# All pairwise products of each row: the whole input loaded by SyncE ahead of the first store, in place of loads that GpSimd issues between the stores

## The chip, the cores and the metric

The kernel runs on one core of one Trainium2 chip. The metric is the device time of one execution in microseconds (us). Three timed runs of the kernel before gave 1261.1, 1260.95 and 1261.11 us; the median is 1261.1 us.

## The reference

For each of 4096 rows of 256 float32 numbers, the reference forms all products of two elements of the row and keeps the upper triangle, diagonal included:

```
dot = jnp.einsum('bi,bj->bij', inputs, inputs)     # inputs: 4096 x 256, f32
iu, ju = jnp.triu_indices(256)
return dot[:, iu, ju]                               # 4096 x 32896, f32
```

The input is 4.19 MB, the output 538.97 MB.

## The kernel before

**Layout.** The 4096 rows stand on the 128 partitions, 32 consecutive rows on each, so that a partition's input is one run of 32 KB. `REPEAT = 2` rows of each partition are worked on at a time (512 input numbers, `each`). The 32,896 output columns are cut into three pieces of 10,944, 10,944 and 11,008 columns (`spans`). One piece for 2 rows on 128 partitions is one store of 256 runs of 43,776 or 44,032 bytes, about 11.2 MB. A pass `h` handles four rows of each partition, 4 KB of input per partition, in six pieces (`p` from 0 to 5); there are eight passes, so 48 pieces in all. `ROUND` says which 4 KB of the input each pass takes.

**Buffers.** Two output buffers, `o0` and `o1` (the list `places`), take turns. A piece is written into one of them by VectorE (helper `vector`, the multiplications of line 281) and GpSimd (helper `gpsimd`, line 382) together, while SyncE's store of the other buffer is on its way. SyncE issues each store in program order (helper `sync`, line 410) once the counter `v_done` says that the piece is complete. VectorE's first multiplication of a piece waits until the earlier store from that buffer has landed (semaphore `free`); GpSimd's first waits for VectorE's (`go`).

**The head.** The first two pieces are done differently (`ahead`). VectorE (line 242) and ScalarE (line 309) write the first piece in blocks, each of which is stored as soon as both are through with it. `FIRST = [704, 1984, 3968, 6592]` gives the borders, so the blocks are 704, 1280, 1984, 2624 and 4352 columns wide. Before block number `DIRECT` VectorE copies the input rows to PSUM (`xp`, line 237). TensorE, which has nothing else to do, counts the landings of the blocks' stores (`head`) and then frees `o0` (line 448).

**The input.** All of it stays in one buffer, `xt` (named `x` in the trace). SyncE loads three parts ahead of the first store (lines 440 and 441): 2 KB per row of the layout, that is per partition, for the first two rows; 8 KB, passes 1 and 2, as 256 runs of 4 KB; 2 KB, the rest of pass 0. Passes 3 to 7 are loaded by GpSimd between its pieces (helper `late`, lines 327 and 354, with the table `LATE`): passes 3 and 4 together (unit `ONE`) and passes 6 and 7 together (unit `TWO`) each in four transfers over 20, 45, 3 and 60 partitions, pass 5 (`EVEN`) in one transfer over all 128. Ahead of most of these GpSimd issues a transfer of 2 to 12 partitions by 2 x 128 bytes into `marks`, a buffer that no instruction reads (helper `mark`). `HAD` makes GpSimd wait, one or two pieces later, until a unit has landed.

Of the kernel before, what the change touches and what calls it, by code (L numbers as in the profile page):

```python
# [8 lines left out]
F32 = mybir.dt.float32  # L9
# [3 lines left out]
P = 128  # L13
UNIT = 64
REPEAT = 2
PIECES = 3
EDGE = 32
ROUND = [0, 2, 5, 1, 3, 7, 4, 6]
GAP = 32
ONE, EVEN, TWO = (3, 4), (5,), (6, 7)  # L20
LATE = [
    ((1, 3), ONE, [((5,), 20), ((6,), 45)]),
    ((2, 3), ONE, [((2,), 3), ((12,), 60)]),
    ((3, 3), EVEN, [((), 128)]),
    ((4, 3), TWO, [((8, 9), 20), ((6,), 45)]),
    ((5, 3), TWO, [((2,), 3), ((12,), 60)]),
]
HAD = [((2, 5), ONE, 4, 0), ((4, 5), EVEN, 1, 0), ((5, 5), TWO, 4, 9)]
HELPED = 1
HELP = 16.5  # L30
MARK = 32
PLACES = 2
SETS = 5
PASS = 6
# [1 line left out]


LATER = 1.0
FIRST = [704, 1984, 3968, 6592]
DIRECT = 3  # L40
COPY = 700


# [94 lines left out]
def window(ap: bass.AP, free: list) -> bass.AP:  # L138
    return bass.AP(ap.tensor, ap.offset, [list(ap.ap[0]), *free])
# [3 lines left out]
def kernel(  # L143
# [15 lines left out]
    nc = tc.nc  # L159
    n, d = x.shape  # L160
    width = out.shape[1]
    each, groups = REPEAT * d, n // (P * REPEAT)
    rounds = PASS // PIECES
    passes = groups // rounds
# [6 lines left out]
    x_in = x.rearrange("(p g) d -> p (g d)", p=P)  # L171
    x_out = out.rearrange("(p h q r) c -> h q p r c", p=P, q=rounds, r=REPEAT)

    pool = ctx.enter_context(tc.tile_pool(name="all", bufs=1))
    edge = pool.tile([P, EDGE], F32, name="edge")
    places = [pool.tile([P, REPEAT, slot], F32, name=f"o{k}") for k in range(PLACES)]
    xt = pool.tile([P, passes, rounds * each + GAP], F32, name="x")
    xv = pool.tile([P, each + 1], F32, name="xv")
    marks = pool.tile([P, 2, 2 * MARK], F32, name="marks")

    xp = ctx.enter_context(tc.tile_pool(name="psum", bufs=1, space=bass.MemoryType.PSUM)).tile([P, each], F32, name="xp")
    ctx.enter_context(tc.tile_critical())  # L182
# [1 line left out]
    def semaphore(name: str):  # L184
        return ctx.enter_context(nc.semaphore(name))

    free = [semaphore(f"free{k}") for k in range(PLACES)]
    head, v_done, a_done, go = (semaphore(s) for s in ("head", "v_done", "a_done", "go"))
    loaded = [semaphore(f"loaded{k}") for k in range(3)]
    far, marked = {u: semaphore(f"far{u[0]}") for u in (ONE, EVEN, TWO)}, semaphore("marked")  # L190

    def take(engine, sem, value: int):
        engine.wait_ge(sem, value).then_inc(sem, -value)  # L193
# [2 lines left out]
    g_done, x_copied, warm = (semaphore(s) for s in ("g_done", "x_copied", "warm"))  # L196

    def x_of(h, q: int) -> bass.AP:
        return xt[:, bass.ds(h, 1), q * each : (q + 1) * each].rearrange("p o d -> p (o d)")

    def blocks(p: int, ahead: bool):

# [99 lines left out]

    def scalar(pieces: range):

        xa = xt[:, 0, :each]
        for p in pieces:
            for _, _, block, _, lo in blocks(p, True):
                todo = [
                    nc.scalar.activation(  # L309
                        places[p][:, r, at - lo : at - lo + length],  # L310
                        xa[:, r * d + j : r * d + j + length],
                        AF.Copy,
                        scale=xa[:, r * d + i : r * d + i + 1],
                    )
                    for i, j, at, length in block
                    for r in range(REPEAT)
                ]
                if todo:
                    todo[-1].then_inc(a_done, 1)
                else:  # L320
                    nc.scalar.sem_inc(a_done, 1)

    flat = xt.rearrange("p h d -> p (h d)")

    def mark(lo: int, hi: int):
        of = window(x_in[lo:hi], [[2 * MARK, 2], [1, MARK]])
        nc.gpsimd.dma_start(marks[lo:hi, :, :MARK], of).then_inc(marked, 16)  # L327

    def inputs(of_passes: tuple, rows: slice, lo: int = 0, hi: int = rounds * each) -> tuple:
        first, last = of_passes[0], of_passes[-1]  # L330
        ends = []
        for ap, at, step in (
            (flat, first * (rounds * each + GAP), (last - first) * (rounds * each + GAP)),
            (x_in, ROUND[first] * rounds * each, (ROUND[last] - ROUND[first]) * rounds * each),
        ):
            dims = [[step, 2], [1, hi - lo]] if step else [[1, hi - lo]]
            ends.append(window(ap[rows, at + lo :], dims))
        return tuple(ends)

    def late(h, p: int):  # L340
        at, rows = 0, {}
        for (begun, piece), of_units, parts in LATE:
            with ExitStack() as when:
                if p == piece:
                    when.enter_context(nc.gpsimd.If(h == begun))
                for steps, count in parts:
                    row = rows.get(of_units, 0)
                    rows[of_units] = row + count
                    for step in steps:
                        if p == piece:  # L350
                            mark(at, at + step)
                        at += step
                    if p == piece:
                        nc.gpsimd.dma_start(*inputs(of_units, slice(row, row + count))).then_inc(far[of_units], 16)  # L354
        for (had, piece), of_units, count, count_of_marks in HAD:
            if p == piece:
                with nc.gpsimd.If(h == had):
                    nc.gpsimd.wait_ge(far[of_units], 16 * count)
                    if count_of_marks:
                        nc.gpsimd.wait_ge(marked, 16 * count_of_marks)  # L360
                    nc.gpsimd.drain()

    def gpsimd(h, pieces: range, ahead: bool, done: int = 0, turns: int = 0) -> tuple:
        if ahead:
            take(nc.gpsimd, go, 1)
            nc.gpsimd.memset(xv[:, each:], 0.0).then_inc(g_own, 1)  # L366
            nc.gpsimd.tensor_copy(xv[:, :each], x_of(0, 0)).then_inc(g_own, 1)  # L367
            done += 2
            nc.gpsimd.wait_ge(g_own, done).then_inc(x_copied, 1)
        for p in [HELPED] if ahead else pieces:  # L370
            place = places[p % PLACES]
            block, lo = helped(p) if ahead else next((block, lo) for _, _, block, _, lo in blocks(p, False))
            turns += not ahead
            if not ahead:
                late(h, p)
            order = interleave(block)
            waits = schedule(order)
            counted = {*waits.values()}
            number = {k: done + 1 + c for c, k in enumerate(sorted(counted))}
            for k, ((i, j, at, length), m, _) in enumerate(order):  # L380
                at -= lo
                ins = nc.gpsimd.tensor_tensor(  # L382
                    place[:, :, at : at + m * length],
                    window(xv[:, j:], [[d, REPEAT], [1, m], [1, length]]),
                    window(xv[:, i:], [[d, REPEAT], [1, m], [0, length]]),
                    ALU.mult,
                )
                if k == 0 and not ahead:
                    ins._wait_ge(go, turns)
                elif k in waits:  # L390
                    ins._wait_ge(g_own, number[waits[k]])
                if k in counted:
                    ins.then_inc(g_own, 1)
            done += len(counted)
            ins.then_inc(g_done, 1)
        return done, turns

    def sync():
        done = ahead_done = 0
        for turn in range(passes * PASS):  # L400
            h, p = divmod(turn, PASS)
            ahead, place = turn < AHEAD, places[p % PLACES]
            parts = list(blocks(p, ahead))
            for lo, hi, *_, base in parts:
                done += 1
                if ahead:
                    ahead_done += 1
                    nc.sync.wait_ge(a_done, ahead_done)
                to = x_out[ROUND[h], p // PIECES, :, :, base + lo : base + hi]
                store = nc.sync.dma_start(to, place[:, :, lo:hi])  # L410
                store._wait_ge(v_done, done)
                store.then_inc(free[p % PLACES] if len(parts) == 1 else head, 16)
        for sem, count in ((v_done, done), (a_done, ahead_done)):
            nc.sync.sem_inc(sem, -count)
# [22 lines left out]
            nc.vector.wait_ge(v_own, counts[0]).then_inc(v_done, 1)  # L437
        settle(engine, counts)

    for (of_passes, lo, hi), sem in zip((((0,), 0, each), ((1, 2), 0, 2 * each), ((0,), each, 2 * each)), loaded):  # L440
        nc.sync.dma_start(*inputs(of_passes, slice(0, P), lo, hi)).then_inc(sem, 16)
    nc.vector.memset(edge, 0.0).then_inc(warm, 1)  # L442
    take(nc.scalar, warm, 1)
    nc.scalar.activation(edge[:, :1], edge[:, 1:2], AF.Copy, scale=edge[:, 2:3])  # L444
    for engine in (nc.vector, nc.scalar, nc.gpsimd):
        engine.wait_ge(loaded[0], 16)
    take(nc.tensor, head, 16 * (len(FIRST) + 1))
    nc.tensor.sem_inc(free[0], 16)
# [35 lines left out]
```

## Time and profile before

| what | value |
|---|---|
| timed runs, median (lowest to highest) | 1261.1 us (1260.95 to 1261.11) |
| profiled execution: span from the first to the last instruction | 1259.5 us |
| VectorE busy | 822.7 us (65%), 1236 instructions |
| GpSimd busy | 763.5 us (61%), 1149 instructions |
| ScalarE busy | 27.1 us (2%), 74 instructions |
| moved by DMA | 543.24 MB, mean 431 GB/s |
| HBM read and written | 4.21 MB and 538.97 MB |

One execution was profiled. Its time is known as the span; the median of the timed runs is 1.6 us longer than the span. The core has 16 DMA engines, which carry out the transfers of all queues: q1 is SyncE's queue, q0 is GpSimd's, q14 fetches instructions. In the views, DVE is VectorE, ACT is ScalarE, POOL is GpSimd, SP is SyncE; a "q" behind an engine is its sequencer, which waits and issues. `L281` is line 281 of the kernel.

### The profile page before, as it was taken

What the parts mean: (1) busy time and instruction counts of PE and PEld (TensorE: products, weight loads), DVE (VectorE), ACT (ScalarE), POOL (GpSimd) and SP (SyncE); (2) the same over time, 40 slices, a digit from 0 to 9 for tenths busy, and PEclk for the clock granted to TensorE, in tenths of its full rate; (3) what the DMA queues carried; (4) which work ended last, traced back from release to release, by engine and by line L of the source; (5) the groups of instructions that cost most, each with busy time, mean ns of one, the idle gap of its engine ahead of it and who ended that gap; (6) DMA issues with size and microseconds to landing.
All of it is one profiled execution on the core that took longest, in us unless ns stands there. A gap on an engine that the chain in (4) does not pass through costs nothing. (4 is left out here: it accounts for less than half of the span.)

```text
span 1259.5 us, 2827 instructions
## 1 busy us (share of the span) xinstructions
DVE 822.7 (65%) x1236; ACT 27.1 (2%) x74; POOL 763.5 (61%) x1149
## 2 busy tenths in 40 slices
DVE  8767657676576665766657675676656766567650
ACT  8000000000000000000000000000000000000000
POOL 5666647665476654766558665576645765467650
DMA  9999999999999999999999999999999999999998
GB/s 396 433 445 423 443 427 433 433 442 427 434 436 432 430 434 435 434 430 441 427 438 433 426 438 427 441 428 438 431 437 428 440 428 437 432 435 432 438 431 380
DMA packets 15911, 543.24 MB, mean 431 GB/s; under 512 B 1440, under 2 KB 1440, under 8 KB 3360
## 3 DMA queue, kind: packets, MB, share of 16 engines
q1 hardware_dynamic: 14704, 540.54, 99.3%
q0 software_dynamic: 1200, 2.64, 0.5%
q14 instruction: 7, 0.06, 0.0%
HBM read 4.21 MB, written 538.97 MB: 431 GB/s over the span
## 5 line engine op out<-in xcount | busy, mean ns | idle before, releaser
L281 DVE TENSOR_TENSOR o<-xv,xp 128x504 f32<-128x504 f32 (+59 forms) x1175 | 791.2, 746 | 398.1 <-DMA out_dram<-o 268.2
L382 POOL TENSOR_TENSOR o<-xv 128x64 f32<-128x64 f32 (+61 forms) x1125 | 751.6, 709 | 450.0 <-DVE o L281 449.8
L309 ACT ACTIVATE o<-x 128x198 f32<-128x198 f32 (+34 forms) x72 | 25.5, 448 | 0.8 <-DMA x<-in_r_inputs_dram 0.8
L260 DVE COPY xp<-x 128x512 f32 x15 | 10.3, 685 | 0.0
L242 DVE TENSOR_TENSOR o<-x,xp 128x470 f32<-128x470 f32 (+18 forms) x19 | 9.7, 585 | 0.0
L242 DVE TENSOR_TENSOR o<-x 128x510 f32<-128x510 f32 (+9 forms) x10 | 5.7, 647 | 2.5 <-DMA x<-in_r_inputs_dram 2.5
L258 DVE COPY xv<-x 128x512 f32 x15 | 6.5, 433 | 0.5
L366 POOL MEMSET xv<- 128x1 f32 x1 | 0.1, 99 | 10.3 <-POOLq L193 10.3
L327 POOL DMA_DIRECT2D marks<-in_r_inputs_dram x9 | 5.7, 637 | 0.4 <-issue 0.3
L354 POOL DMA_DIRECT2D x<-in_r_inputs_dram x9 | 5.5, 615 | 0.0
L444 ACT ACT_TABLE_LOAD x1 | 1.3, 1283 | 1.2 <-ACTq L193 1.2
L442 DVE MEMSET edge<- 128x32 f32 x1 | 0.1, 85 | 1.0 <-SPq L182 1.0
L237 DVE COPY xp<-x 128x512 f32<-128x512 f32 x1 | 0.7, 686 | 0.0
L367 POOL COPY xv<-x 128x512 f32<-128x512 f32 x1 | 0.6, 611 | 0.0
L444 ACT ACTIVATE edge<-edge 128x1 f32<-128x1 f32 x1 | 0.3, 295 | 0.0
L471 POOL MEMSET const-float32-0.0<- 128x1 f32 x1 | 0.1, 99 | 0.2 <-issue 0.2
L471 POOL MEMSET const-bfloat16-1.0<- 128x1 bf16 x1 | 0.1, 103 | 0.0
L471 POOL MEMSET const-uint8-127<- 128x1 uint8 x1 | 0.1, 103 | 0.0
L471 POOL MEMSET const-float32-1.0<- 128x1 f32 x1 | 0.1, 99 | 0.0
## 6 DMA issues: line engine op xcount, KB each, us to landing
out_dram<-o SPq DMA_DIRECT2D x31, 10944.0 KB, 35.2
out_dram<-o SPq DMA_DIRECT2D x16, 11008.0 KB, 32.8
out_dram<-o SPq DMA_DIRECT2D x1, 4352.0 KB, 13.8
out_dram<-o SPq DMA_DIRECT2D x1, 2624.0 KB, 9.4
out_dram<-o SPq DMA_DIRECT2D x1, 1984.0 KB, 7.2
out_dram<-o SPq DMA_DIRECT2D x1, 1280.0 KB, 5.2
x<-in_r_inputs_dram SPq DMA_DIRECT2D x1, 1024.0 KB, 4.9
x<-in_r_inputs_dram POOLq DMA_DIRECT2D x2, 480.0 KB, 29.2
```

The source lines that it names most:

```text
L237: nc.vector.tensor_copy(xp, x_of(h, 0)).then_inc(v_own, 1)
L242: ins = nc.vector.tensor_tensor(place[:, :, at - lo : at - lo + length], window(x_of(h, 0)[:, j:], [[d, REPEAT], [1, 1], [1, length]]), wi ...
L258: ins = nc.vector.tensor_copy(xv[:, :each], x_of(h, p // PIECES))
L260: nc.vector.tensor_copy(xp, x_of(h, p // PIECES)).then_inc(v_own, 1)
L281: ins = nc.vector.tensor_tensor(place[:, :, at : at + m * length], window(xv[:, j:], [[d, REPEAT], [1, m], [1, length]]), window(xp[:, i:] ...
L309: nc.scalar.activation(places[p][:, r, at - lo : at - lo + length], xa[:, r * d + j : r * d + j + length], AF.Copy, scale=xa[:, r * d + i ...
L327: nc.gpsimd.dma_start(marks[lo:hi, :, :MARK], of).then_inc(marked, 16)
L354: nc.gpsimd.dma_start(*inputs(of_units, slice(row, row + count))).then_inc(far[of_units], 16)
L367: nc.gpsimd.tensor_copy(xv[:, :each], x_of(0, 0)).then_inc(g_own, 1)
L382: ins = nc.gpsimd.tensor_tensor(place[:, :, at : at + m * length], window(xv[:, j:], [[d, REPEAT], [1, m], [1, length]]), window(xv[:, i:] ...
L444: nc.scalar.activation(edge[:, :1], edge[:, 1:2], AF.Copy, scale=edge[:, 2:3])
L471: nc = _bacc.Bacc("TRN2", target_bir_lowering=False, num_devices=1)
```

## The change

SyncE loads all input in two transfers ahead of the first store: 2 KB per partition as before, and then the remaining 30 KB per partition as one run. `late`, `mark`, `inputs` and their tables go, and so do GpSimd's 18 transfers, its waits for them and `ROUND`: pass `h` now takes the `h`-th 4 KB. The first piece is stored in two blocks of 3968 and 6976 columns, with the copy to PSUM ahead of the second.

```
-ROUND = [0, 2, 5, 1, 3, 7, 4, 6]
-GAP = 32
-ONE, EVEN, TWO = (3, 4), (5,), (6, 7)
-LATE = [
-    ((1, 3), ONE, [((5,), 20), ((6,), 45)]),
-    ((2, 3), ONE, [((2,), 3), ((12,), 60)]),
...
-HAD = [((2, 5), ONE, 4, 0), ((4, 5), EVEN, 1, 0), ((5, 5), TWO, 4, 9)]
...
-FIRST = [704, 1984, 3968, 6592]
-DIRECT = 3
+FIRST = [3968]
+DIRECT = 1
...
-    xt = pool.tile([P, passes, rounds * each + GAP], F32, name="x")
+    xt = pool.tile([P, groups * each], F32, name="x")
...
-            if not ahead:
-                late(h, p)
...
-                to = x_out[ROUND[h], p // PIECES, :, :, base + lo : base + hi]
+                to = x_out[h, p // PIECES, :, :, base + lo : base + hi]
...
-    for (of_passes, lo, hi), sem in zip((((0,), 0, each), ((1, 2), 0, 2 * each), ((0,), each, 2 * each)), loaded):
-        nc.sync.dma_start(*inputs(of_passes, slice(0, P), lo, hi)).then_inc(sem, 16)
+    for (lo, hi), sem in zip(((0, each), (each, groups * each)), loaded):
+        nc.sync.dma_start(xt[:, lo:hi], x_in[:, lo:hi]).then_inc(sem, 16)
```

SyncE's queue at the start of the program, before. `x_61` is the input buffer, `o0_59` and `o1_60` are the two output buffers; shapes are partitions x runs x elements:

```order
L441 DMA x_61<-in_r_inputs_dram 128x512
L441 DMA x_61<-in_r_inputs_dram 128x2x1024
L441 DMA x_61<-in_r_inputs_dram 128x512
L441 UNCONDITIONAL_BRANCH
L410 DMA out_0_dram<-o0_59 128x2x704 [waits a_done,v_done]
L410 DMA out_0_dram<-o0_59 128x2x1280 [waits a_done,v_done]
L410 DMA out_0_dram<-o0_59 128x2x1984 [waits a_done,v_done]
L410 DMA out_0_dram<-o0_59 128x2x2624 [waits a_done,v_done]
L410 DMA out_0_dram<-o0_59 128x2x4352 [waits a_done,v_done]
L410 DMA out_0_dram<-o1_60 128x2x10944 [waits a_done,v_done]
```

And after:

```order
L385 DMA x_61<-in_r_inputs_dram 128x512
L385 DMA x_61<-in_r_inputs_dram 128x7680
L385 UNCONDITIONAL_BRANCH
L354 DMA out_0_dram<-o0_59 128x2x3968 [waits a_done,v_done]
L354 DMA out_0_dram<-o0_59 128x2x6976 [waits a_done,v_done]
L354 DMA out_0_dram<-o1_60 128x2x10944 [waits a_done,v_done]
```

The 30 KB runs stand ahead of the first store on the same queue, and the first piece is stored by two transfers instead of five; the 47 stores behind it are the same.

GpSimd's queue in the loop before, from the end of piece 2 on. Each group of transfers stands under a branch that takes it in one pass alone (of the five groups, the first two are shown):

```order
L382 TENSOR_TENSOR o0_59<-xv_62 128x2
L345 COMPARE_AND_BRANCH
L327 DMA marks_63<-in_r_inputs_dram 5x2x32
L354 DMA x_61<-in_r_inputs_dram 20x2x1024
L327 DMA marks_63<-in_r_inputs_dram 6x2x32
L354 DMA x_61<-in_r_inputs_dram 45x2x1024
L343 UNCONDITIONAL_BRANCH
L345 COMPARE_AND_BRANCH
L327 DMA marks_63<-in_r_inputs_dram 2x2x32
L354 DMA x_61<-in_r_inputs_dram 3x2x1024
L327 DMA marks_63<-in_r_inputs_dram 12x2x32
L354 DMA x_61<-in_r_inputs_dram 60x2x1024
```

And after, from the same place:

```order
L326 TENSOR_TENSOR o0_59<-xv_62 128x2
L326 TENSOR_TENSOR o1_60<-xv_62 128x2x454 [waits go]
L326 TENSOR_TENSOR o1_60<-xv_62 128x2x448
L326 TENSOR_TENSOR o1_60<-xv_62 128x2x442
L326 TENSOR_TENSOR o1_60<-xv_62 128x2x432
```

All 18 transfers have left GpSimd's queue, and the multiplications of piece 3 follow those of piece 2 directly.

More of the change, by code (lines that the diff above doesn't have):

```diff
@@ L17 @@
 EDGE = 32
-ROUND = [0, 2, 5, 1, 3, 7, 4, 6]
-GAP = 32
-ONE, EVEN, TWO = (3, 4), (5,), (6, 7)
-LATE = [
-    ((1, 3), ONE, [((5,), 20), ((6,), 45)]),
-    ((2, 3), ONE, [((2,), 3), ((12,), 60)]),
[L24 to L27, printed above, removed]
-HAD = [((2, 5), ONE, 4, 0), ((4, 5), EVEN, 1, 0), ((5, 5), TWO, 4, 9)]
 HELPED = 1
 HELP = 16.5
-MARK = 32
 PLACES = 2
@@ L176 @@
     places = [pool.tile([P, REPEAT, slot], F32, name=f"o{k}") for k in range(PLACES)]
-    xt = pool.tile([P, passes, rounds * each + GAP], F32, name="x")
+    xt = pool.tile([P, groups * each], F32, name="x")
     xv = pool.tile([P, each + 1], F32, name="xv")
-    marks = pool.tile([P, 2, 2 * MARK], F32, name="marks")
     xp = ctx.enter_context(tc.tile_pool(name="psum", bufs=1, space=bass.MemoryType.PSUM)).tile([P, each], F32, name="xp")
@@ L188 @@
     head, v_done, a_done, go = (semaphore(s) for s in ("head", "v_done", "a_done", "go"))
-    loaded = [semaphore(f"loaded{k}") for k in range(3)]
-    far, marked = {u: semaphore(f"far{u[0]}") for u in (ONE, EVEN, TWO)}, semaphore("marked")
+    loaded = [semaphore(f"loaded{k}") for k in range(2)]
     def take(engine, sem, value: int):
@@ L198, in x_of @@
     def x_of(h, q: int) -> bass.AP:
-        return xt[:, bass.ds(h, 1), q * each : (q + 1) * each].rearrange("p o d -> p (o d)")
+        return xt[:, bass.ds(h * (rounds * each) + q * each, each)]
     def blocks(p: int, ahead: bool):
@@ L303, in scalar @@
     def scalar(pieces: range):
-        xa = xt[:, 0, :each]
+        xa = xt[:, :each]
         for p in pieces:
@@ L321, in scalar @@
                     nc.scalar.sem_inc(a_done, 1)
[L323 to L361, printed above, removed]
     def gpsimd(h, pieces: range, ahead: bool, done: int = 0, turns: int = 0) -> tuple:
```

## The prediction

> **What bounds the kernel now.** I read the page first, for the share of the DMA engines, their queues and the chain that ended last.
>
> ```profile
> DMA  9999999999999999999999999999999999999998
> DMA packets 15911, 543.24 MB, mean 431 GB/s; under 512 B 1440, under 2 KB 1440, under 8 KB 3360
> q1 hardware_dynamic: 14704, 540.54, 99.3%
> q0 software_dynamic: 1200, 2.64, 0.5%
> L281 DVE TENSOR_TENSOR o<-xv,xp 128x504 f32<-128x504 f32 (+59 forms) x1175 | 791.2, 746 | 398.1 <-DMA out_dram<-o 268.2
> L382 POOL TENSOR_TENSOR o<-xv 128x64 f32<-128x64 f32 (+61 forms) x1125 | 751.6, 709 | 450.0 <-DVE o L281 449.8
> ```
>
> The 16 DMA engines have no empty slice. VectorE is idle for 398 us, most of it waiting for stores, and GpSimd for 450 us behind VectorE. So neither compute engine sets the end, and an instruction saved on GpSimd is worth nothing. What counts is bytes over rate, and within that the engine of the 16 that finishes last, because a landing counts only when all 16 are through.
>
> That last point needs a closer view: the timeline of VectorE. Each row is a group of instructions from its start; the 35 multiplications that begin with 128x260 start when the third store before has landed on all engines (in brackets, the idle time and what ended it). Such a row comes once in three stores.
>
> ```profile
> 190.33 18.18 DVE L281 TENSOR_TENSOR o<-xv,xp 128x260 f32<-128x260 f32 x35 [9.29 <-DMA out_dram<-o]
> ...
> 894.97 18.18 DVE L281 TENSOR_TENSOR o<-xv,xp 128x260 f32<-128x260 f32 x35 [9.42 <-DMA out_dram<-o]
> 972.62 18.18 DVE L281 TENSOR_TENSOR o<-xv,xp 128x260 f32<-128x260 f32 x35 [9.30 <-DMA out_dram<-o]
> 1050.26 18.18 DVE L281 TENSOR_TENSOR o<-xv,xp 128x260 f32<-128x260 f32 x35 [9.43 <-DMA out_dram<-o]
> 1128.22 18.18 DVE L281 TENSOR_TENSOR o<-xv,xp 128x260 f32<-128x260 f32 x35 [9.43 <-DMA out_dram<-o]
> 1206.22 18.18 DVE L281 TENSOR_TENSOR o<-xv,xp 128x260 f32<-128x260 f32 x35 [9.52 <-DMA out_dram<-o]
> ```
>
> The last four steps are 77.65, 77.64, 77.96 and 78.00 us, though each holds the same three stores and no load. The last engine to land became 0.35 us per three stores slower. Nothing in the program changes there. What fits is one engine that is always 0.35 us (0.45%) slower per three stores and that was hidden until about 1050 us, because others with a fixed delay landed after it.
>
> The end of the trace shows the 16 engines apart. These are windows of time; the last two columns are the share of the DMA engines and GB/s, and a packet is counted where it starts.
>
> ```profile
> 1254.00:1254.50 0.50, 0.00 (x0) 0.00 (x0) 0.00 (x0) 1.00 0.61 264
> 1254.50:1255.00 0.50, 0.00 (x0) 0.00 (x0) 0.00 (x0) 1.00 1.63 705
> 1255.00:1255.25 0.25, 0.00 (x0) 0.00 (x0) 0.00 (x0) 1.00 0.82 352
> 1255.25:1255.50 0.25, 0.00 (x0) 0.00 (x0) 0.00 (x0) 1.00 0.81 352
> 1255.50:1255.75 0.25, 0.00 (x0) 0.00 (x0) 0.00 (x0) 1.00 0.00 0
> ...
> 1256.00:1256.25 0.25, 0.00 (x0) 0.00 (x0) 0.00 (x0) 1.00 0.42 176
> ```
>
> At 43,776 bytes per packet, 264 GB/s over 0.5 us are 3 packets, 705 are 8, 352 over 0.25 us are 2, twice, and 176 are 1: sixteen last packets. Fifteen start at 1254.8 on the mean of the windows' middles, one alone at 1256.1, so 1.3 us later. But 48 stores at 0.35 us per three would have put the slow engine 16 x 0.35 = 5.6 us behind. So 4.3 us have been given back to it, and only something that loads the engines unevenly can do that.
>
> The stores load them evenly (256 equal runs each). The input does not. Here are its transfers, with KB of each and the time from issue to landing:
>
> ```profile
> x<-in_r_inputs_dram SPq DMA_DIRECT2D x1, 1024.0 KB, 4.9
> x<-in_r_inputs_dram POOLq DMA_DIRECT2D x2, 480.0 KB, 29.2
> x<-in_r_inputs_dram POOLq DMA_DIRECT2D x2, 360.0 KB, 30.1
> x<-in_r_inputs_dram SPq DMA_DIRECT2D x2, 256.0 KB, 3.8
> x<-in_r_inputs_dram POOLq DMA_DIRECT2D x1, 512.0 KB, 19.7
> x<-in_r_inputs_dram POOLq DMA_DIRECT2D x2, 160.0 KB, 16.1
> x<-in_r_inputs_dram POOLq DMA_DIRECT2D x2, 24.0 KB, 11.2
> ```
>
> Those of 480, 360, 160 and 24 KB, two each, are units `ONE` and `TWO`: 60, 45, 20 and 3 partitions. 45 and 60 divide by 15 and not by 16, 20 and 3 reach still fewer engines evenly. Together they are 2 x 1024 KB = 2.10 MB; spread evenly at 431 GB/s that would be 4.87 us per engine. An engine left out of all of it is spared 4.87 us, and 4.3 us is what the two views above ask for. I conclude that the slow engine carries between nothing and 0.6 us of it. The Trainium skill has a rule for this ("DMA: Bandwidth & Descriptors", "Why a DMA increments its semaphore by 16 and not by 1"): a transfer takes the largest count of engines up to 16 that divides its slowest dimension, and GpSimd's transfers take consecutive engines from a cursor that goes round. By that rule 45 and 60 partitions leave one engine out and the small `marks` transfers choose which; the sum would be the one with nothing carried, +4.3 us below. No view here shows the engines by number.
>
> **The change, part by part.** The rates at the start of the program come from windows of 1, 1, 2, 3 and 4 us:
>
> ```profile
> 2.00:3.00 1.00, 0.00 (x0) 0.81 (x2) 0.00 (x0) 1.00 0.89 266
> 4.00:5.00 1.00, 1.00 (x3) 1.00 (x5) 0.00 (x0) 1.00 0.99 401
> 5.00:7.00 2.00, 2.00 (x5) 2.00 (x7) 0.00 (x0) 1.00 1.02 401
> 7.00:10.00 3.00, 2.96 (x7) 3.00 (x10) 0.00 (x0) 1.00 1.04 428
> 10.00:14.00 4.00, 4.00 (x9) 4.00 (x12) 2.98 (x4) 1.00 1.02 431
> ```
>
> Runs of 2 to 5 KB go at 401 GB/s, those from 8 KB up at 428 to 431.
>
> *The loads, on the slow engine.* Removed: the three loads of the start, 1.57 MB at 401 GB/s, 3.92 us; the even 512 KB transfer, 0.52 MB at 431, 1.22 us; of `ONE` and `TWO`, 0 to 0.6 us. Added: 2 KB runs, 0.26 MB at 401, 0.65 us; 30 KB runs, 3.93 MB. The trace has no load in runs that long. Its nearest rows are 401 GB/s (loads of 2 and 4 KB) and 431 (stores of 43,776 bytes): 9.81 or 9.12 us. I take 9.12, since 30 KB is nearer to 43 KB and the rate rises with the run. The net is 9.77 - 5.14 = +4.63 us with nothing carried, +4.0 with 0.6.
>
> *The first piece in two blocks.* The runs of 704 and 1280 columns, 2.03 MB at 401 GB/s, become runs of 16 and 28 KB at 431: 5.06 - 4.71 = -0.35 us. Three issues less cost the path nothing, since the engines are full then.
>
> *Does the DMA run dry in the head?* SyncE, ScalarE and VectorE start so:
>
> ```profile
> 0.96 1.38 SPq L441 DMA_DIRECT2D x<-in_r_inputs_dram  x3
> 3.61 5.71 DVE L242 TENSOR_TENSOR o<-x 128x510 f32<-128x510 f32 x10 [2.49 <-DMA x<-in_r_inputs_dram]
> 3.61 25.49 ACT L309 ACTIVATE o<-x 128x256 f32<-128x256 f32 x72 [0.79 <-DMA x<-in_r_inputs_dram]
> 9.24 0.69 DVE L237 COPY xp<-x 128x512 f32<-128x512 f32 x1
> 9.96 9.66 DVE L242 TENSOR_TENSOR o<-x,xp 128x470 f32<-128x470 f32 x19
> 34.39 18.18 DVE L281 TENSOR_TENSOR o<-xv,xp 128x260 f32<-128x260 f32 x35 [5.36 <-PEq L448]
> 60.32 15.40 DVE L281 TENSOR_TENSOR o<-xv,xp 128x1024 f32<-128x1024 f32 x16 [6.15 <-DMA out_dram<-o]
> ```
>
> The first block now has 9 multiplications with 4394 elements per partition, where the 10 before had 4738: 5.71 x 4394/4738 = 5.3 us, done at 8.9. ScalarE has 14 of its 72 instructions in it, 5.0 us by count and 6.1 by their greater width, done at 8.6 to 9.7. The first load was issued at 0.96 and moved from 2.0 on, 1 us later; so the first store is ready by 10.7 at the latest. The 30 KB load is through at 3.0 + 9.1 = 12.1. The store waits 1.4 us in the queue, and the engines do not run dry. The second block (a copy of 0.69 and 18 multiplications, about 9.5 us) is done at 19.2 on VectorE, and ScalarE needs about as long; it moves from 20.5, while the first store lasts until 12.1 + 4.06 MB/431 = 21.5. A margin of 1 us. The third store was issued by about 29.5 and the second lasts to 21.5 + 16.6 = 38.1. So zero, with 1 us as the bound if ScalarE is late.
>
> *Buffer `o0` comes free later*, at about 38.5 in place of 34.39. The multiplications then take 18.18 us, to 57, while the third store runs until 64. Before, 34.39 + 18.18 = 52.6 stood against the landing at 60.32. The cover of 7 us is the same, so this costs nothing.
>
> *GpSimd.* Its 18 issues and three waits stand where it waits for VectorE anyway (450 us idle). Nothing gained.
>
> Sum: +4.63 - 0.35 = +4.3 us, or +3.7 with 0.6 carried. I take +4.1, nearer the end that the divisors speak for. The sum is made on the profiled execution, 1259.5 us, which comes to 1263.6; the timed runs lie 1.6 us above the span, for work around it that does not change: 1261.1 + 4.1 = **1265.2 us**, 0.33% slower.
>
> **The rivals.**
>
> *A, the slow engine gets its full share (the forecast).* For it speak the steps that grow without a load and the last packet that stands alone. Its own range is 1263.8 to 1266.2: drift of 0.32 to 0.36 per three stores, and 0.7 for slower load runs.
>
> *B, not slower: no engine is slow in the changed kernel.* If the lag comes with GpSimd's transfers, or with recording the profile alone, all 16 engines simply carry the same bytes. From 190.33 to 894.97 there are nine steps, 704.64 us; at 77.65 that would be 698.85, so GpSimd's loads cost 5.79 us on the last engine. With 3.92 for the head that is 9.71, against 9.77 after, and -0.35 for the blocks: 1260.8, or 1260.1 if the lone packet goes too (1.3 us, less the 0.5 by which the later of the others lag their mean). Against its first form: the load rows below end by 836.4 + 31.8 = 868.2 us, and the step grew after 1050.
>
> ```profile
> L354 POOL DMA_DIRECT2D x<-in_r_inputs_dram x9: 577/624/655, 209.4 to 836.4; - x9
> DMA to landing us min/median/max: 11.1/19.7/31.8
> ```
>
> The second form cannot be told from one profiled execution. The Trainium skill ("DMA: Bandwidth & Descriptors", "Latency and other measured facts") says that engines 7 and 15 are usually slower in traces, and guesses at contention with GpSimd's descriptor rings, which SyncE's transfers do not use; by that guess the changed kernel would come out at 1260.1. The trace agrees that an engine is slow and, by the step that grew 180 us after GpSimd's last landing, not with the guess. B decides where the drift falls below 0.25 per three stores, since each 0.05 less takes 0.8 us off and 2.5 us are 0.2%.
>
> *C, the long load is slow or leaves a gap.* At the 266 GB/s of its first microsecond 3.93 MB would take 14.8 us, 5.7 more, so with A 1270.9. Against it: the rate is over 400 by 4 us.
>
> *D, faster: loads amid stores cost more than their bytes.* 2.62 MB at 431 are 6.08 us and the steps show 5.79, so there is no surcharge to win back. It would take 2.5 us, to 1258.5 or less.
>
> **How the numbers follow.** A measurement of this kernel tells a change of about 0.2% (2.5 us) from none. A has 0.70, all slower; a drift half hidden, with 1262 to 1263.5, 0.07, the same; B 0.16, the same; C 0.04, slower; D 0.03, faster. So slower 0.74, same 0.23, faster 0.03. The range reaches from B's upper figures to A's upper end, 1260.7 to 1266.3.
>
> **What would show it.** Right: VectorE's 128x260 rows stand 78.0 apart, from about 300 us to the end, not 77.65; the last packet of one engine starts 5 us or more after the other fifteen, so that the last windows show a share of 0.06; the span is near 1263.6. The head is right if no window between 3 and 40 us falls below 400 GB/s. Wrong: steps of 77.65 throughout and a common end (B); windows with a share under 0.9 between 9 and 25 us (C); first block stored after 12 us. If the span grows by 4 us and the timed runs do not, the slow engine belongs to the profile.

## The result and the profile after

The changed kernel takes 1264.92 us (median of 7 runs, 1264.48 to 1265.18) against 1261.08 for the kernel before on the same chip: 3.84 us more, a ratio of 1.0031 with a 95% interval of 1.0021 to 1.0040. The forecast was 1265.2 us. The span of the profiled execution went from 1259.5 to 1262.8 us.

The page of the changed kernel shows the same load on the DMA engines as before, with nothing left in GpSimd's queue:

```profile
DMA  9999999999999999999999999999999999999997
DMA packets 13623, 543.22 MB, mean 430 GB/s; under 512 B 816, under 2 KB 816, under 8 KB 944
q1 hardware_dynamic: 13616, 543.17, 99.5%
x<-in_r_inputs_dram SPq DMA_DIRECT2D x1, 3840.0 KB, 12.4
```

As many bytes moved, no slice is empty, and yet the end is later. The 40 slices are a mean over 16 engines and cannot show where. The rows of VectorE's timeline that come once in three stores can (start, duration, then the idle time before and what ended it):

```profile
352.33 18.67 DVE L267 TENSOR_TENSOR o<-xv,xp 128x260 f32<-128x260 f32 x36 [9.31 <-DMA out_dram<-o]
429.99 18.67 DVE L267 TENSOR_TENSOR o<-xv,xp 128x260 f32<-128x260 f32 x36 [9.43 <-DMA out_dram<-o]
507.63 18.67 DVE L267 TENSOR_TENSOR o<-xv,xp 128x260 f32<-128x260 f32 x36 [9.32 <-DMA out_dram<-o]
585.55 18.67 DVE L267 TENSOR_TENSOR o<-xv,xp 128x260 f32<-128x260 f32 x36 [9.54 <-DMA out_dram<-o]
663.57 18.67 DVE L267 TENSOR_TENSOR o<-xv,xp 128x260 f32<-128x260 f32 x36 [9.43 <-DMA out_dram<-o]
...
1131.67 18.67 DVE L267 TENSOR_TENSOR o<-xv,xp 128x260 f32<-128x260 f32 x36 [9.44 <-DMA out_dram<-o]
1209.65 18.67 DVE L267 TENSOR_TENSOR o<-xv,xp 128x260 f32<-128x260 f32 x36 [9.52 <-DMA out_dram<-o]
```

The steps are 77.66 and 77.64 us up to 507.63, then 77.92, 78.02 and so on; the eight from 585.55 to 1209.65 take 624.10 us, 78.01 each. In the kernel before, such steps of 78 us began at 1050. Here they begin some 500 us earlier, as they would if the same slow engine had become the last that much sooner.

The last windows of the trace (the last two columns are the share of the DMA engines and GB/s; a packet is counted where it starts):

```profile
1253.00:1254.00 1.00, 0.00 (x0) 0.00 (x0) 0.00 (x0) 1.00 1.02 440
1254.00:1255.00 1.00, 0.00 (x0) 0.00 (x0) 0.00 (x0) 1.00 0.81 352
1255.00:1256.00 1.00, 0.00 (x0) 0.00 (x0) 0.00 (x0) 1.00 0.11 44
1256.00:1257.00 1.00, 0.00 (x0) 0.00 (x0) 0.00 (x0) 1.00 0.20 88
1257.00:1258.00 1.00, 0.00 (x0) 0.00 (x0) 0.00 (x0) 1.00 0.10 44
1258.00:1259.00 1.00, 0.00 (x0) 0.00 (x0) 0.00 (x0) 1.00 0.00 0
1259.00:1260.00 1.00, 0.00 (x0) 0.00 (x0) 0.00 (x0) 1.00 0.10 44
```

44 GB/s over 1 us is one packet of 44 KB. From 1255 on only five packets start, and the last, after 1259, stands alone: one engine still has three packets to move, 1.6 us each (44,032 bytes at a sixteenth of 431 GB/s), when nearly all the others are through.

### The profile page after: what moved, and what is told of

Read it like the earlier page. It is cut to its first block, busy times and chain, and to the rows that moved or that the text cites. A ratio compares the mean times of both kernels' runs of the same rounds, so it can differ in the third digit from the quotient of the medians.

```text
span 1262.8 us, 2727 instructions
## 1 busy us (share of the span) xinstructions
DVE 821.9 (65%) x1234; ACT 27.1 (2%) x72; POOL 751.5 (60%) x1131
## 5 line engine op out<-in xcount | busy, mean ns | idle before, releaser
L295 ACT ACTIVATE o<-x 128x256 f32<-128x256 f32 (+34 forms) x70 | 25.5, 457 | 1.0 <-DMA x<-in_r_inputs_dram 1.0
L228 DVE TENSOR_TENSOR o<-x,xp 128x454 f32<-128x454 f32 (+17 forms) x18 | 9.4, 599 | 0.0
L228 DVE TENSOR_TENSOR o<-x 128x498 f32<-128x498 f32 (+8 forms) x9 | 5.3, 658 | 2.7 <-DMA x<-in_r_inputs_dram 2.7
```

Of the source, the lines that this page charges most:

```text
L228: ins = nc.vector.tensor_tensor(place[:, :, at - lo : at - lo + length], window(x_of(h, 0)[:, j:], [[d, REPEAT], [1, 1], [1, length]]), wi ...
L295: nc.scalar.activation(places[p][:, r, at - lo : at - lo + length], xa[:, r * d + j : r * d + j + length], AF.Copy, scale=xa[:, r * d + i ...
```

## The experiments

All are compared with the kernel before on the same chip, whose medians were 1260.72 to 1260.91 us. The theory (A) is that of the forecast: one DMA engine is slower than the others, and the kernel before spared it most of the input. The rivals put the loss into the head of the program (H), or into loading ahead of the stores rather than between them (G).

**Spread alone.** The kernel before, with `ONE` and `TWO` loaded evenly:

```
-    ((1, 3), ONE, [((5,), 20), ((6,), 45)]),
-    ((2, 3), ONE, [((2,), 3), ((12,), 60)]),
+    ((1, 3), ONE, [((), 128)]),
     ((3, 3), EVEN, [((), 128)]),
-    ((4, 3), TWO, [((8, 9), 20), ((6,), 45)]),
-    ((5, 3), TWO, [((2,), 3), ((12,), 60)]),
+    ((4, 3), TWO, [((), 128)]),
...
```

(The counts in `HAD` follow the number of transfers, here and in the tries further down.)

> The kernel before, with units ONE and TWO loaded by GpSimd in one transfer each over all 128 partitions and without the marks; same bytes, same passes, same queue, so only the spread over the 16 DMA engines changes. Theory A (one DMA engine is 0.36 us per three stores slower and the uneven loads spared it): 1264.5 to 1266, steps of VectorE's 128x260 rows of 78.0 us from the middle of the run on, and a last packet that stands 4 us or more behind the other fifteen. Rival H (the loss of the change lies in its head: longer load ahead of the first store, two blocks): 1261.1, as before. Rival G (loads between the stores are better than ahead of them, whatever their spread): 1261.1.

Measured: 1264.79 us against 1260.72, 4.07 more (ratio 1.0031, 1.0020 to 1.0043). Head, five blocks and passes are those of before, and GpSimd still loads between the stores, so H and G are not needed to lose these 4 us. That 15 fewer transfers are issued is left to the next experiment. The trace has the marks of A: steps of 78.0 from 425.81 on wherever no load falls into a step (with a load they are 79 to 80.5), and a late, lone packet:

```profile
425.81 18.18 DVE L279 TENSOR_TENSOR o<-xv,xp 128x260 f32<-128x260 f32 x35 [9.50 <-DMA out_dram<-o]
503.84 18.18 DVE L279 TENSOR_TENSOR o<-xv,xp 128x260 f32<-128x260 f32 x35 [9.42 <-DMA out_dram<-o]
...
1131.79 18.18 DVE L279 TENSOR_TENSOR o<-xv,xp 128x260 f32<-128x260 f32 x35 [9.43 <-DMA out_dram<-o]
1209.78 18.18 DVE L279 TENSOR_TENSOR o<-xv,xp 128x260 f32<-128x260 f32 x35 [9.47 <-DMA out_dram<-o]
```

```profile
1258.00:1259.00 1.00, 0.00 (x0) 0.00 (x0) 0.00 (x0) 1.00 0.10 44
1259.00:1260.00 1.00, 0.00 (x0) 0.00 (x0) 0.00 (x0) 1.00 0.10 44
```

**Uneven, but another engine spared.** The kernel before, one number changed:

```
-    ((1, 3), ONE, [((5,), 20), ((6,), 45)]),
+    ((1, 3), ONE, [((13,), 20), ((6,), 45)]),
```

> The kernel before with 13 partitions in place of 5 in the first transfer into marks, nothing else (1 KB more is read). If GpSimd's transfers go to consecutive engines from a cursor, all the later ones move by 8 engines, and another engine is left out. Theory A: the slow engine now carries its share and more, 1265.5 to 1267, with steps of 78.0 us and a lone tail. Rival (uneven loads as such, or GpSimd's small transfers as such, are what helps): 1261.1.

Measured: 1265.88 us, 5.16 more (1.0040, 1.0026 to 1.0055). The loads are as uneven as before, there are as many transfers, and the bytes differ by 2 KB (not the 1 KB of the expectation); what is left to decide is which engine is left out. That the number of partitions in a transfer whose data nobody reads costs 5 us is the clearest sign that the later transfers go to engines by a running cursor. It is what the Trainium skill states ("DMA: Bandwidth & Descriptors", "Why a DMA increments its semaphore by 16 and not by 1"), and these times agree with it.

**Is it the engine, or the traffic around it?** The changed kernel, with the products of the loop cut to one column each:

```
+                    length = length if ahead else 1
                     ins = nc.vector.tensor_tensor(
...
+                length = length if ahead else 1
                 ins = nc.gpsimd.tensor_tensor(
```

(The last 64 columns of both buffers are set to zero once, so that every store has something to read.)

> The changed kernel with every multiplication of the loop cut to one column (all but the first two pieces), so that VectorE and GpSimd issue the same instructions but hardly touch the buffers; the stores and the load are the same, the output is not the reference's. Theory A (the slow engine is slow by itself): the lone last packet stands 5 us or more behind the others as in the changed kernel, the span is 1262 to 1263.5. Rival (the lag comes from VectorE's and GpSimd's traffic to the buffers): a common end, 1258 to 1259.5.

Measured, one run: 1265.22 us, span 1263.1. VectorE is busy for 144.3 us in place of 821.9 and GpSimd for 185.0 in place of 751.5, and the slow engine is as slow:

```profile
DVE 144.3 (11%) x1236; ACT 27.1 (2%) x72; POOL 185.0 (15%) x1131
```

```profile
975.91 2.99 DVE L268 TENSOR_TENSOR o<-xv,xp 128x2 f32<-128x2 f32 x35 [23.10 <-DMA out_dram<-o]
1053.91 2.99 DVE L268 TENSOR_TENSOR o<-xv,xp 128x2 f32<-128x2 f32 x35 [23.20 <-DMA out_dram<-o]
1131.94 3.00 DVE L268 TENSOR_TENSOR o<-xv,xp 128x2 f32<-128x2 f32 x35 [23.10 <-DMA out_dram<-o]
1209.94 2.99 DVE L268 TENSOR_TENSOR o<-xv,xp 128x2 f32<-128x2 f32 x35 [23.19 <-DMA out_dram<-o]
```

The steps are 78.00, 78.03 and 78.00 us. So the lag does not come from VectorE's and GpSimd's traffic to the buffers, nor from GpSimd's transfers, since this kernel has none. It stands in the stores themselves. (This is one execution; its steps agree with the changed kernel's, and its span is 0.3 us longer.)

**The two blocks alone.** The kernel before with the changed kernel's blocks:

```
-FIRST = [704, 1984, 3968, 6592]
-DIRECT = 3
+FIRST = [3968]
+DIRECT = 1
```

> The kernel before with the first piece in two blocks of 3968 and 6976 columns, nothing else. The first store is then issued near 9.6 us, while the loads of the head are through at 7. Theory A: the DMA engines stand idle for some 3 us before the first store, and the end comes about that much later less 0.35 for the longer runs: 1263.5 to 1264.5; steps and tail as before. Rival H, in the form that two blocks alone are free: 1261.0. In the changed kernel that gap is covered by the long load.

Measured: 1266.29 us, 5.57 more (1.0042, 1.0026 to 1.0059), 1.8 us above the expectation's upper end. The windows show the gap that was expected, and a second one between the two blocks:

```profile
6.00:7.00 1.00, 1.00 (x3) 1.00 (x4) 0.00 (x0) 1.00 0.43 164
7.00:10.00 3.00, 2.96 (x6) 3.00 (x9) 0.00 (x0) 1.00 0.00 0
10.00:13.00 3.00, 3.00 (x7) 3.00 (x9) 2.35 (x4) 1.00 0.99 423
19.50:20.50 1.00, 1.00 (x2) 1.00 (x5) 1.00 (x2) 1.00 0.05 16
```

They come to 0.57 + 3 + 0.95, about 4.5 us without work for the DMA engines. With the 0.35 us that the longer runs should save, some 1.4 us of the 5.57 are not accounted for. In the changed kernel both gaps are covered: the 30 KB load is on the engines until the first block is ready, and thereby the first store lasts until the second block is. The two edits of the change belong together; the second without the first would cost more than the whole change does.

**The long load with five blocks.**

```
-FIRST = [3968]
-DIRECT = 1
+FIRST = [704, 1984, 3968, 6592]
+DIRECT = 3
```

> The changed kernel with the first piece in five blocks again; the long load stays ahead of them. Theory A by the packets' rates: 0.35 us more than the changed kernel for the shorter runs, 1265.2 to 1265.4. If the two blocks cost something that the long load does not cover: less than 1264.9.

Measured: 1265.47 us, 4.64 more than before (1.0034, 1.0022 to 1.0047), against 3.84 for the changed kernel. That is 0.8 us more where 0.35 was expected, and the intervals are wider than this difference. Nor is it the blocks' alone: from 3 to 13 us, which is the long load, this run's engines moved 367 GB/s where the changed kernel's moved 392:

```profile
3.00:13.00 10.00, 9.37 (x17) 9.40 (x27) 2.00 (x4) 1.00 0.99 367
```

Over 10 us that is 0.25 MB, or 0.6 us. What the two blocks save behind the long load is not separated.

**Sparing the last-numbered engine in the head.** The changed kernel, its 30 KB load cut in two:

```
-        nc.sync.dma_start(xt[:, lo:hi], x_in[:, lo:hi]).then_inc(sem, 16)
+        for a, b in [(0, P)] if lo == 0 else [(0, 120), (120, P)]:
+            nc.sync.dma_start(xt[a:b, lo:hi], x_in[a:b, lo:hi]).then_inc(sem, 16)
...
```

(The waits count both parts.)

> The changed kernel with the 30 KB load cut into 120 and 8 partitions. If a SyncE transfer over 120 partitions takes the 15 lowest-numbered engines and one over 8 the 8 lowest, the last engine carries none of it and is spared 9.1 to 10 us, the others carry 0.6 to 1.3 us more. Theory A with the last engine as the slow one: the slow engine comes out ahead, the end is set by the next latest, 1261.5 to 1263. Theory A with another slow engine: 1265.5 to 1266.5. Rival H: 1264.9, or a little more for the longer load.

Measured: 1277.52 us (1.0133, 1.0116 to 1.0150), far outside every expectation. For most of the load the engines moved little more than half of the changed kernel's 392 GB/s (shown further down), though they were busy:

```profile
4.00:24.00 20.00, 19.97 (x34) 20.00 (x55) 13.16 (x13) 1.00 0.97 215
```

In the trace's single packets a run of 30 KB takes 2.4 us here at the median, against 1.15 in the changed kernel. Why is open. So the time says nothing on which engine is slow; it says what this one split costs.

**Looking for a better version.** `EVEN` is the one unit that the slow engine still shares in the kernel before. Three tries, each with `EVEN` in 60, 60 and 8 partitions, and one with the transfers of 20 moved:

```
 first:   ((3, 3), EVEN, [((1,), 60), ((1,), 60), ((1,), 8)])       and TWO's (8, 9) -> (8,)
 second:  ((3, 3), EVEN, [((8, 9), 60), ((8, 9), 60), ((8, 9), 8)]) and TWO's (8, 9) -> (8,)
 third:   ((3, 3), EVEN, [((), 60), ((), 60), ((), 8)])
 fourth:  ONE, [((10,), 20), ((1,), 45)]    TWO, [((8, 14), 20), ((1,), 45)]
```

The first:

> The kernel before with unit EVEN loaded in transfers of 60, 60 and 8 partitions, with marks of one partition that put the cursor where it stands ahead of the transfers of 45 and 60, in place of one over all 128. Theory A: the slow engine is spared up to 1.27 us more and no longer ends alone; the next latest stands 0.9 us ahead of it, so the end comes 0.6 to 0.9 us earlier, 1260.0 to 1260.4. If the lone last packet is not what sets the time: no change, 1260.7 to 1261.1.

The fourth:

> The kernel before with the two transfers of 20 partitions moved by 5 engines (10 and 1 partitions in the marks around the first of them, 8 and 14, and 1, around the second), those of 45 and 60 and 3 left where they were. If the slow engine carried two partitions of each 20 (two thirds of a microsecond each), it is now spared them or not, by where it stands: spared, the end comes up to 0.9 us earlier, 1260.0 to 1260.4. If it carried none and still carries none: 1260.7 to 1261.1. If it carries them only now: 1262.

Measured: 1263.62 us (1.0021, 1.0012 to 1.0030) and 1265.08 us (1.0032, 1.0019 to 1.0044), both slower. I had taken a mark of one partition to move the cursor by one. By the Trainium skill's rule in the section named above it moves by two, since the slowest dimension that is not of size 1 is then its two runs. That would account for the fourth: 45 and 60 then leave out another engine in both units. For the first it was to be seen with other marks:

> Again the kernel before with unit EVEN in transfers of 60, 60 and 8 partitions, now with marks of 8 and 9 partitions ahead of each, which move the cursor by 17, that is by one, where a mark of one partition moves it by two (its slowest dimension above 1 is the two runs). So 45 and 60 leave out the same engine as in the kernel before, in all units. Theory A: the slow engine is spared up to 1.27 us more, the next latest stands 0.9 us ahead of it: 1260.0 to 1260.4. If the cursor does not move so: 1262 to 1264, as with the marks of one partition.

Measured: 1263.73 us (1.0023, 1.0014 to 1.0032), as with the marks of one partition. So the marks' shape was not the reason there, and the transfers of 60 with one run per partition came under suspicion:

> The kernel before with unit EVEN in transfers of 60, 60 and 8 partitions and no marks ahead of them; ONE and TWO with their marks as before. It asks whether a transfer of 60 partitions with one run each moves the cursor. If it does not (it would then always use the same 15 engines): TWO still spares the slow engine, and the time is that of before, 1260.6 to 1261.2, or 1260.0 to 1260.4 if the engine left out is the slow one. If it does: TWO leaves out another engine, as in the two tries with marks, 1263.4 to 1264.

Measured: 1261.36 us against 1260.91 (1.0003, 0.9994 to 1.0012), no difference that can be told. The time is as if these transfers, other than those with two runs, did not move the cursor, so that in the first two tries the marks alone had carried it off for `TWO`. Losing `TWO` alone costs 2.8 to 2.9 us in both, losing both units 4.1 to 5.2: the cost goes with what the slow engine has to carry. In the third try the lone packet at the end is gone:

```profile
1254.00:1255.00 1.00, 0.00 (x0) 0.00 (x0) 0.00 (x0) 1.00 1.12 484
1255.00:1256.00 1.00, 0.00 (x0) 0.00 (x0) 0.00 (x0) 1.00 0.71 308
1256.00:1257.00 1.00, 0.00 (x0) 0.00 (x0) 0.00 (x0) 1.00 0.01 0
```

Seven packets start after 1255 and none after 1256. The median does not gain from it, and the profiled execution (1260.85 us) is the fastest of that kernel's eleven. No version tried beats the kernel before.

**The packets one by one.** The kept traces hold every DMA packet with its start, length and bytes, but not its engine. A packet starts 3 to 4 ns before the one ahead of it on its engine ends. Joined end to start, the 12,032 store packets of 43 KB of a kernel therefore fall into 16 chains of about 752. (Where two chains end within a few ns of each other they can be confused; the slow one was followed by its long packets.)

- *One engine is slow, all the time.* In the changed kernel 11,487 of the packets took exactly 1618 or 1627 ns, by their size. Another 542 took up to 60 ns longer, 5.8 us in all, and 5.6 us of this lies in one chain, spread over the whole run. That chain ends 5.3 us after the mean of the other fifteen, and 3.3 us after the latest of them.
- *The kernel before spares it `ONE` and `TWO` entirely.* There the slow chain holds 35 KB of what GpSimd loads: 32 KB of `EVEN`, the rest marks. With the spread loads it holds 164 KB, with the shifted cursor more than 180 KB, and in the first try with `EVEN` nothing of `ONE` and all of `TWO`.
- *The transfers of 60 partitions with one run leave out the same engine twice.* In the third try one chain has none of `EVEN`'s packets, so the cursor stood still between them. It is not the slow chain, which holds 37 KB of `EVEN`, more than before. So the third try did not relieve the slow engine, and why its last packet does not stand alone there is open.

## Why the prediction was right

*The bound.* Bytes over rate on the engine that ends last: right. The two views that carried it, steps that grow without a load and a lone last packet, came back stronger, and the spread experiment reproduces the loss without the rest of the change.

*The relief that is lost.* The term was 4.87 us, less 0 to 0.6 that the slow engine carries anyway. The spread experiment measures 4.07, so the term looks too large by 0.8, and its own lower end, 4.27, was missed by 0.2; the interval of that run, 2.5 to 5.4 us, holds all of these. The packets say what it consists of. The slow engine carried nothing of `ONE` and `TWO`, so the 0 was right and the 0.6 had nothing to stand on. GpSimd's packets took 6.42 us of its time with the spread loads and 1.95 before, 4.47 in place of 4.87. Against this, some of its store packets took over 60 ns too long in the kernel before, 1.15 us in all, and none did with the spread loads; most such packets of that kernel lie beside GpSimd's transfers. That makes 3.3 of the 3.6 us between the two profiled spans.

*The head.* The changed kernel is 0.23 us better off (3.84 - 4.07) than evenly spread loads with the old head. By the prediction's terms that was 9.77 for the loads of the head, less 3.92 and 6.09 (1.22 + 4.87) for the old ones, less 0.35 for the blocks: -0.59. The term that was clearly mis-sized is the 30 KB load. I took the rate of the long stores, 431 GB/s, but between 3 and 13 us it ran at 392, full engines throughout:

```profile
3.00:13.00 10.00, 9.14 (x17) 9.17 (x25) 2.21 (x4) 1.00 1.00 392
```

3.93 MB at 392 GB/s are 10.0 us in place of 9.12. The other end of my bounds, 9.81 at the rate of the short loads, was the better guess. The length of the run was still a fair argument for most packets: half of the 128 took 1153 ns or less, which on 16 engines is 426 GB/s. The mean is 1261 ns because some, nearly all at the start and between 10 and 12 us, took up to 2024; why is open. The load's 0.9 us alone would have made the head +0.3, so about 0.5 us went the other way. Of that, 0.3 is that GpSimd's spread loads took 6.42 us of the slow engine's time where the terms make it 6.09; the rest is not separated. The head's test was also badly put. I had said that no window would fall below 400 GB/s; with packets of over 1 us counted where they start, short windows swing far more than that, and this one is under 400.

*Sum.* -0.8 on the relief and +0.4 on the head: 4.3 became 3.84, and the taken value of 4.1 lay between. That it came nearer than 4.3 is luck: the 0.2 was taken off for a share of `ONE` and `TWO` that the slow engine does not carry, and two errors of the other terms cancelled in part.

*No gap in the head, and `o0` free later at no cost.* Right in effect. VectorE got `o0` at 41.47 us, 3 later than the forecast 38.5:

```profile
9.58 20.24 SPq L354 DMA_DIRECT2D out_dram<-o  x3
41.47 18.67 DVE L267 TENSOR_TENSOR o<-xv,xp 128x260 f32<-128x260 f32 x36 [12.87 <-PEq L392]
67.09 15.40 DVE L267 TENSOR_TENSOR o<-xv,xp 128x1024 f32<-128x1024 f32 x16 [5.90 <-DMA out_dram<-o]
```

About 1 us of it is the load. With 18.67 us of work it is done at 60.1, and the store in front of it lands at 67.09, when VectorE's next row starts. The first store was issued at 9.58, within the forecast 8.9 to 9.7.

*The steps.* They turned to 78.0 at 507 us and not at 300: other engines with a fixed delay hide the slow one longer than I had supposed. Its lag at the end is the lag of the whole run all the same. The other sign, a last packet 5 us or more behind the other fifteen, holds for their mean (5.3 us) and not for the latest of them (3.3).

*The rivals.* B's first form, that the lag comes with GpSimd's transfers, is refuted by the changed kernel itself, which has none. Its second form, that the profile makes the lag, falls with the timed runs: they lost 3.84 us where the span lost 3.3. The guess of the Trainium skill on engines 7 and 15, which it calls usually slower in traces ("DMA: Bandwidth & Descriptors", "Latency and other measured facts"), is contention with GpSimd's descriptor rings. It does not account for this lag either, which is there without GpSimd's transfers; that an engine is slow agrees, and whether it is 7 or 15 no view shows. C had something in it (the load is 0.9 us longer than taken) but left no gap. Its sign, a window under 0.9, is met literally by short windows (0.11 from 12 to 13 us), for the reason just given; from 9 to 25 us the share is 1.02. D had nothing.

## What to carry to other kernels

In a kernel that is bound by DMA, the time is that of the DMA engine that ends last, and equal bytes on 16 engines are not equal times: look at single packets in the last windows, and at steps between equal events for one that grows. A transfer that looks clumsy because it covers 45 or 60 partitions may be doing the balancing, as it did here, so before it is tidied away, work out what each engine carries. When a load is moved ahead of the first store, what it covers counts as much as what it costs: here it made room for coarser first blocks, which alone left the engines idle for about 4.5 us.

## What the runs showed of the hardware that was not expected

One of the 16 DMA engines moves the stores about 0.45% slower than the rest (steps of 78.0 us in place of 77.65), in the profiles of the kernels here, whether VectorE and GpSimd are busy for 65 and 60% of the span or for 11 and 15%. Over 48 stores this is more than 5 us. The experiments ran on three chips, and the kernel before, whose loads spare that engine, had medians of 1260.72 to 1260.91 us on all of them. What makes it slow is open.

With a SyncE load over 120 partitions and one over 8, in place of one over 128, the engines moved 215 GB/s in place of 392, with their share of busy time at 0.97. What slows the packets was not tried.

GpSimd's transfers over 60 partitions moved the cursor when they had two runs per partition and, by the times, did not when they had one: 1263.7 us with marks around them and 1261.4 without, where the rule that fits two runs would have had it the other way round.
